# Destination one-hots kept in DRAM by two passes and loaded by two later ones, in a four-layer graph network

## The chip, the cores and the metric

The kernel runs on one core of a Trainium2 chip. The metric is the device time of one execution in microseconds. Engines: PE (TensorE, matmuls, with its weight loads shown apart as PEld), DVE (VectorE), ACT (ScalarE), POOL (GpSimd), SP (SyncE, which issues the DMAs).

## What is computed

The input is a graph of 12,500 nodes and 200,000 edges (`src`, `dst`, a type and a weight per edge) and a 64-wide feature `x` per node. Four layers follow each other, each with a residual and a layer norm. Cut to what matters here:

```python
# layer 0: two hyperbolic hops over the edges (per-edge arithmetic, then a mean by src)
x = _layernorm(x + _L0_gnn_ref(x, relation_emb, edge_index, edge_type))
# layer 1: two rounds; messages are summed by src, from rows gathered by dst, then a GRU cell
agg = segment_sum(messages, row, N); x = gru_cell(agg, x, ...)
# layer 2: two SAGE convolutions, 16 wide inside; rows gathered by src, mean by dst
h   = relu(segment_sum(x[src], dst, N) * inv_deg @ W1_l + b1 + x @ W1_r)
out =      segment_sum(h[src], dst, N) * inv_deg @ W2_l + b2 + h @ W2_r
# layer 3: two SAGE convolutions, 64 to 128 to 64, the same gather and mean
```

So layers 1 to 3 are six sums over all edges: two that gather by dst and add by src (layer 1), four that gather by src and add by dst (layers 2 and 3).

## The kernel before, in words

The setup sorts the edges into a 49 x 49 grid. A cell (k, j) holds the edges whose summing node lies in group k and whose gathered node lies in group j (256 nodes to a group); each cell is one tile of at most 128 edges. There are 49 x 49 = 2401 tiles. For each tile two short vectors are kept: the gathered node's place as a row in DRAM (`d_rows`, `s_rows`) and the summing node's place as a column in SBUF (`slc` by src, `dlc` by dst, one column of 128 values per tile). Then come the two hops of layer 0 (L1332, `hyper_hop`), which also make one-hots: the first hop stores them in DRAM (L1366, L1451) and the second loads them (L1368, L1453).

The change lies in the six passes at the end (`sum_pass`, L1659), called at L1942 to L1947: passes 0 and 1 are layer 1, passes 2 and 3 layer 2, passes 4 and 5 layer 3. A pass walks the 2401 tiles in 172 steps of PG = 14 tiles (the last has 7). For each step `prepare` (L1669) does this:

- a DMA brings the rows of the 14 tiles, broadcast to all partitions (`row`, 448 KB, L1671);
- two DVE tensor_scalars compare them with the partition's number: `o`, the one-hots by gathered node, for each half of a group (L1676);
- one DVE tensor_tensor compares `iota_r` with the tiles' columns: `s`, the one-hots by summing node, [128, 256 nodes, 14 tiles] with the tile innermost (L1678).

PE uses them in two kinds of matmul. `gather` (L1682) multiplies `o` with the table of node values (kept in three bf16 parts, so 3 x 64 = 192 columns; in layer 2 3 x 16 = 48, or 49 with a count) into the PSUM tile `pg` (L1690), and ACT casts it to `gb` (L1696). `scatter` (L1699) multiplies a tile's `s` with its `gb` and adds into `ps`, one PSUM bank for each k (L1704). A gather block has 2 tiles with 192 columns and 7 tiles with 48 or 49; a scatter follows two blocks later, or one.

When the last tile of a k has been added, the node work of that k (a generator such as `gru_node`, L1769) goes into a queue, and `tick` (L1652) issues a piece of it every second time: DVE reduces `ps` (L1727), in layer 1 makes the second half of `u` (L1777), PE transposes (L1781), ACT copies and activates, and so on to the table of the next pass.

The order on PE, DVE, ACT and POOL is the order in which this Python code issues the instructions (`manual_schedule`, L1637). The order on SP, which issues all DMAs, is chosen by the framework's scheduler. `row`, `o` and `s` have two buffers each. The preparation of step i+1 is issued among the gathers of step i.

## Time and profile before

| | us |
|---|---|
| median of 3 runs (12247.88 to 12251.74) | 12251.63 |
| the profiled execution's own time | 12251.38 |
| its span in the trace | 12249.7 |
| layer 0 and setup, to the first gather of pass 0 | 7090.9 |
| passes 0 and 1 (layer 1) | 982 and 1131 |
| passes 2 and 3 (layer 2) | 610 and 697 |
| passes 4 and 5 (layer 3), to the end of the span | 926 and 813 |

The profile is one execution, taken by the hardware profiler. "Busy" is the time in which an engine works on at least one instruction. Consecutive instructions of DVE overlap a little in it, so an instruction's duration is somewhat longer than the time from its start to the start of the next. A wait is the idle time of an engine before an instruction, put down to the instruction that released it. The granted clock is the share of TensorE's full clock that the throttle allowed; over the whole execution it was 0.922. A name such as "o<-row,iota_p" says what an instruction writes and reads; L1676 is line 1676 of the kernel.

### The profile page before, as it was taken

Reading aid. Unit: us, or ns where it says so; the run is one execution under the profiler, and the core shown is the slowest. Engines: PE = TensorE matmul, PEld = TensorE weight load, DVE = VectorE, ACT = ScalarE, POOL = GpSimd, SP = SyncE. Lnnn points to the kernel's source line nnn. Section 1 sums busy time; section 2 is a strip of 40 time slices with the busy share of each in tenths; the row PEclk is TensorE's granted clock in tenths of the full one; section 3 lists DMA queues with packets and bytes.
Section 4 is the critical chain, followed back from the end, with each engine's and each line's share of the span. In section 5 each row is a group of like instructions: output and inputs, shape, how many; then the busy total and the mean of one; then the engine's idle time right before and its main releaser. Section 6 shows DMA issues by size and latency. Waiting matters only on the chain.

```text
span 12249.7 us, 360176 instructions
## 1 busy us (share of the span) xinstructions
PE 10426.3 (85%) x147935; PEld 9021.3 (74%) x147935; DVE 9997.8 (82%) x22903; ACT 8238.9 (67%) x22338; POOL 1120.3 (9%) x2806
## 2 busy tenths in 40 slices
PE   6865888888888489999999689999997777999999
PEld 5754666666666377777777479988887777899999
DVE  7877999999999687787777676666669999766788
ACT  4544777777777488888888656667773222566777
POOL 0002222222222011111111000000000000000000
PEclk8777999999999799999999899999997766899999
DMA  1127777777677555555555422222223333222232
GB/s 30 11 27 232 262 263 262 265 262 265 262 264 263 132 213 212 211 210 213 211 212 212 135 78 83 81 76 70 72 70 123 136 116 115 95 88 87 96 105 97
DMA packets 681163, 1903.34 MB, mean 155 GB/s; under 512 B 324353, under 2 KB 327016, under 8 KB 591687
## 3 DMA queue, kind: packets, MB, share of 16 engines
q1 hardware_dynamic: 679494, 1880.19, 44.8%
q8 instruction: 1158, 18.97, 0.6%
q14 instruction: 511, 4.18, 0.1%
HBM read 1294.39 MB, written 585.58 MB: 153 GB/s over the span
## 4 chain that ended last, share of the span: by engine, by line
PE 43%; DVE 38%; ACT 11%; issue 6%; DMA 2%; SPq 0%; ACTq 0%; DVEq 0%; POOL 0%
PE ps L1704 13%; PE pg L1690 12%; DVE q L1407 5%; PE pm L1429 4%; DVE hd L1410 3%; DVE s L1678 3%; DVE o L1676 3%; ACT RS L1424 2%; PE ph L1376 2%; DVE z L1182 2%; ACT L1182 2%; PE po L963 2%; ACT mx L1437 2%; DVE oh L1449 2%; PE ps L1461 2%
## 5 line engine op out<-in xcount | busy, mean ns | idle before, releaser
L1696 ACT CAST gb<-pg 128x384 bf16<-128x384 f32 (+2 forms) x5490 | 2550.4, 474 | 1567.4 <-PE pg L1690 1555.3
L1704 PE MATMUL ps<-gb,s 128*128 128x192 bf16 (+2 forms) x28812 | 3070.3, 240 | 207.7 <-ACT gb L1696 196.3
L1690 PE MATMUL pg<-xs,o 128*128 128x192 bf16 (+2 forms) x28812 | 2849.5, 232 | 156.7 <-DMA row<-d_rows 125.7
L1704 PEld LDWEIGHTS <-s 128*128 128x128 bf16 x28812 | 2529.4, 146 | 277.0 <-issue 246.0
L1690 PEld LDWEIGHTS <-o 128*128 128x128 bf16 x28812 | 2070.8, 102 | 177.8 <-issue 129.9
L1676 DVE TENSOR_SCALAR o<-row,iota_p 128x1792 bf16<-128x1792 f16 x2064 | 1369.2, 681 | 653.4 <-PE pg L1690 643.3
L1376 PEld LDWEIGHTS <-o 128*128 128x128 bf16 x28812 | 1093.4, 100 | 1069.3 <-issue 476.6
L1376 PE MATMUL ph<-hx,o 128*128 128x69 bf16 x28812 | 1166.4, 199 | 685.1 <-DVE o L1363 314.1
L1678 DVE TENSOR_TENSOR s<-iota_r,dlc 128x3584 bf16<-128x3584 f16 x688 | 1391.5, 2023 | 184.1 <-PE ps L1704 183.3
L1437 ACT ACTIVATE mx<-pm 128x448 bf16<-128x448 bf16 x2058 | 1117.7, 544 | 579.3 <-PE pm L1440 574.8
L1424 ACT ACTIVATE HS<-HS,wh 128x64 f32<-128x64 f32 x4802 | 1225.9, 358 | 1.0 <-DVE wh L1182 1.0
L1424 ACT ACTIVATE RS<-RS,wtr 128x64 f32<-128x64 f32 x4802 | 1217.7, 341 | 0.0
L1382 PEld LDWEIGHTS <-o 128*128 128x128 bf16 x28812 | 1082.5, 100 | 115.2 <-issue 60.2
L1382 PE MATMUL pt<-tabx,o 128*128 128x67 bf16 x28812 | 1107.2, 198 | 2.1 <-issue 2.1
L1461 PE MATMUL ps<-mx,oh 128*128 128x196 bf16 (+1 forms) x9604 | 968.1, 254 | 0.0
L1678 DVE TENSOR_TENSOR s<-iota_r,slc 128x3584 bf16<-128x3584 f16 x344 | 696.1, 2024 | 245.6 <-PE ps L1704 243.6
L1461 PEld LDWEIGHTS <-oh 128*128 128x128 bf16 x9604 | 849.1, 134 | 46.1 <-issue 28.8
L1410 DVE TENSOR_REDUCE hd<-q 128x7 f32<-128x448 f32 x1372 | 823.1, 613 | 0.0
L1429 PE MATMUL pm<-HS,ident 128*128 128x448 f32 x1372 | 685.8, 581 | 93.7 <-ACT mx L1437 93.3
L1440 PE MATMUL pm<-mx,nident 128*128 128x448 bf16 x1372 | 498.7, 363 | 249.0 <-ACT mx L1437 249.0
L1429 PE MATMUL pm<-T,ident 128*128 128x448 f32 x1372 | 628.8, 539 | 0.0
L1429 PE MATMUL pm<-RS,ident 128*128 128x448 f32 x1372 | 627.4, 538 | 0.6 <-ACT RS L1424 0.6
(377 smaller groups left out, 15335.7 us busy)
## 6 DMA issues: line engine op xcount, KB each, us to landing
by_node<-o SPq DMA_DIRECT2D x343, 1120.0 KB
o<-by_node SPq DMA_DIRECT2D x343, 1120.0 KB
row<-s_rows SPq DMA_DIRECT2D x684, 448.0 KB
row<-hop_rows SPq DMA_DIRECT2D x343, 672.0 KB
by_edge<-oh SPq DMA_DIRECT2D x343, 448.0 KB
oh<-by_edge SPq DMA_DIRECT2D x343, 448.0 KB
row<-d_rows SPq DMA_DIRECT2D x342, 448.0 KB
heads<-hx SPq DMA_DIRECT2D x14, 724.5 KB
```

What stands on the lines that cost most here:

```text
L1376: pe.matmul(ph[:, t, :], o[:, 2 * q, t, :], head[k][:, q, i * RW : (i + 1) * RW], start=q + i == 0, stop=q + i == 3)
L1382: pe.matmul(pt[:, t, :], o[:, 2 * q + 1, t, :], tabx[:, 2 * (g * HG + t) + q, i * TW : (i + 1) * TW], start=q + i == 0, stop=q + i == 3)
L1410: vec.tensor_reduce(o, q[:, i], AX.X, OP.add)
L1424: act.mul(x[:, t, :], x[:, t, :], coef[k][2 * rels][:, g * HG + t : g * HG + t + 1])
L1429: pe.matmul(pm[n], ident, x, start=i == 0, stop=i == 2, skip_group_check=True)
L1437: act.activation(mx[n][:, :, i * D : (i + 1) * D], x, AF.Relu)
L1461: pe.matmul(ps[k][:, q, :], oh[n][:, q * P : (q + 1) * P, t], mx[n][:, t, :], start=g + t + q == 0, stop=g * HG + t == HT - 1, skip_group_ ...
L1676: ts(o[:, q, :n, :], row[:, :n, :], iota_p[:, q : q + 1], None, OP.is_equal)
L1678: tt(s[:, :, :n], iota_r[:, :, :n], cols_flat[:, t0 : t0 + n].unsqueeze(1).to_broadcast([P, GN, n]), OP.is_equal)
L1690: pe.matmul(pg[:, t, :], o[:, q, jo, :], xs[:, 2 * j + q, 0:wx], start=q == 0, stop=q == 1)
L1696: act.copy(gb[:, : len(js), :], pg[:, : len(js), :])
L1704: pe.matmul(ps[k][:, h, :], s[:, h * P : (h + 1) * P, jo], gb[:, t, :], start=j + h == 0, stop=j == NG - 1, skip_group_check=True)
```

## The change

In passes 0 and 1 a second generator, `keep_one_hots`, runs beside the gathers, one piece per tile. For each k it makes one-hots by destination for the tiles of column k of the later passes' grid that lie in the first seven of their step of 14; pass 0 makes every second one of them and pass 1 the others. Each is one DVE tensor_scalar of 128 x 256 (nodes innermost) with a column of `dlc` as the scalar. Up to four of them are stored by one DMA into `kept`, a DRAM tensor of 172 steps x 128 x 7 x 256.

In passes 2 and 3 (`load=True`) the first seven tiles of each step come from `kept` by one DMA of 448 KB, and only the other seven are made by the tensor_tensor. Passes 4 and 5 make all of them, as before.

In every pass `s` is now laid out in two blocks of seven tiles: a made block is [256 nodes, 7 tiles] with the tile innermost, a loaded block [7 tiles, 256 nodes] with the node innermost. `iota_r` has 7 instead of 14 columns per node, and the tensor_tensor that makes two blocks is one instruction with four dimensions.

```diff
-    iota_r = keep.tile([P, GN, PG], F16, name="iota_r")
+    iota_r = keep.tile([P, GN, HG], F16, name="iota_r")
...
+    iota_n = keep.tile([P, GN], F16, name="iota_n")
+    kept = dram.tile([-(-NG * NG // PG), P, HG, GN], BF16, name="kept")
...
-            s = wp.tile([P, GN, PG], BF16, name="s")
-            ready.append((o, s))
+            s = wp.tile([P, 2, GN * HG], BF16, name="s")
+            by_tile = s[:, 0, :].rearrange("p (t n) -> p t n", n=GN)
+            by_node = s.rearrange("p b (n t) -> p b n t", t=HG)
+            def edges_of(t, h):
+                hs = slice(h * P, (h + 1) * P)
+                return by_tile[:, t, hs] if load and t < HG else by_node[:, t // HG, hs, t % HG]
+            ready.append((o, edges_of))
+            if load:
+                m = min(n, HG)
+                nc.sync.dma_start(out=by_tile[:, :m, :], in_=kept[t0 // PG, :, :m, :])
             for q in range(2):
                 ts(o[:, q, :n, :], row[:, :n, :], iota_p[:, q : q + 1], None, OP.is_equal)
                 yield
-            tt(s[:, :, :n], iota_r[:, :, :n], cols_flat[:, t0 : t0 + n].unsqueeze(1).to_broadcast([P, GN, n]),
-               OP.is_equal)
+            b0, b1 = (1 if load else 0), n // HG
+            if b1 > b0:
+                c = cols_flat[:, t0 + b0 * HG : t0 + b1 * HG].rearrange("p (b t) -> p b t", t=HG)
+                tt(by_node[:, b0:b1], iota_r.unsqueeze(1).to_broadcast([P, b1 - b0, GN, HG]),
+                   c.unsqueeze(2).to_broadcast([P, b1 - b0, GN, HG]), OP.is_equal)
             yield
+
+        def keep_one_hots(k):
+            odd = k % PG >= HG
+            js = range(odd, NG, 2)[keep_half::2]
+            cols = wp.tile([P, NG], F32, name="cols")
+            copy(cols, dlc[:, :, k])
+            yield
+            for i in range(0, len(js), 4):
+                jj = js[i : i + 4]
+                d = wp.tile([P, 4, GN], BF16, name="d")
+                for t, j in enumerate(jj):
+                    ts(d[:, t, :], iota_n, cols[:, j : j + 1], None, OP.is_equal)
+                    yield
+                at = [(j * NG + k) // PG for j in jj]
+                nc.sync.dma_start(out=kept[at[0] : at[-1] + 1 : PG, :, k % HG, :].rearrange("s p n -> p s n"),
+                                  in_=d[:, : len(jj), :])
...
+                if keep_half is not None and j == 0:
+                    side.append(keep_one_hots(k))
+                while side and next(side[0], side) is side:
+                    side.pop(0)
...
-                    pe.matmul(ps[k][:, h, :], s[:, h * P : (h + 1) * P, jo], gb[:, t, :],
+                    pe.matmul(ps[k][:, h, :], s(jo, h), gb[:, t, :],
...
-    sum_pass(0, tabs[0], d_rows, slc, D, gru_node(0))
-    sum_pass(1, tabs[1], d_rows, slc, D, gru_node(1))
-    sum_pass(2, tabs[0], s_rows, dlc, 16, first_mean, extra=1)
-    sum_pass(3, tabs[1], s_rows, dlc, 16, second_mean)
+    sum_pass(0, tabs[0], d_rows, slc, D, gru_node(0), keep_half=0)
+    sum_pass(1, tabs[1], d_rows, slc, D, gru_node(1), keep_half=1)
+    sum_pass(2, tabs[0], s_rows, dlc, 16, first_mean, extra=1, load=True)
+    sum_pass(3, tabs[1], s_rows, dlc, 16, second_mean, load=True)
```

## The prediction

> **What bounds it now.** I read the page for the costliest groups, cut the six summing passes apart by counting the gather's weight loads (4802 to a pass), and took the windows view over these stretches, passes 0 to 5 in order. Columns: microseconds, busy time of PE, weight loads, VectorE (DVE), ScalarE (ACT), GpSimd; granted clock, DMA share, GB/s.

> ```profile
> core 0: us, PE busy (x) PEld busy (x) DVE busy (x) ACT busy (x) POOL busy (x), PEclk, DMA share, GB/s
> 7090.90:8073.00 982.10, 963.83 (x10755) 921.47 (x10756) 668.29 (x945) 634.60 (x1536) 0.00 (x0) 1.00 0.24 82
> 8073.00:9204.00 1131.00, 1021.60 (x11059) 965.49 (x11058) 731.51 (x1468) 816.35 (x1822) 0.00 (x0) 0.99 0.21 71
> 9204.00:9814.00 610.00, 482.88 (x9647) 468.13 (x9644) 587.23 (x943) 171.25 (x463) 0.00 (x0) 0.77 0.39 131
> 9814.00:10511.00 697.00, 547.68 (x9900) 527.60 (x9898) 635.60 (x1048) 204.16 (x581) 0.00 (x0) 0.66 0.34 115
> 10511.00:11437.00 926.00, 904.30 (x10190) 869.39 (x10190) 635.81 (x773) 624.28 (x1498) 0.00 (x0) 1.00 0.26 87
> 11437.00:12249.70 812.70, 798.87 (x9617) 795.04 (x9614) 681.80 (x1010) 587.30 (x1305) 0.00 (x0) 1.00 0.31 101
> ```

> Passes 0, 1, 4, 5 are held by PE (98, 90, 98, 98% busy; DVE 65 to 84%). Passes 2 and 3, where a matmul moves only 48 or 49 columns, are held by DVE (96 and 91%); PE is at 79% there. So DVE time taken from passes 2 and 3 counts nearly in full, and DVE time put into passes 0 and 1 costs only where PE waits for DVE. The waits view of pass 0 shows how much room DVE has there (total us, times, longest):

> ```profile
> DVE o L1676 <- PE pg L1690: 186.2, 123, 2.1
> DVE s L1678 <- PE ps L1704: 114.5, 147, 1.5
> ```

> 301 us in 172 steps, 1.75 us a step.

> **Part 1: the one-hot `s`.** The page's group for s, and the same operation in the first hop with rows of 7 (source view: ns min/median/max):

> ```profile
> L1678 DVE TENSOR_TENSOR s<-iota_r,dlc 128x3584 bf16<-128x3584 f16 x688 | 1391.5, 2023 | 184.1 <-PE ps L1704 183.3
> ```
> ```profile
> L1449 DVE TENSOR_TENSOR oh<-iota_r,slc x343: 1154/1218/1239, 1108.1 to 4104.9; 128x1792 bf16<-128x1792 f16 x172
> ```

> Rows of 14 cost 2023 ns for 3584 elements, rows of 7 cost 1218 for 1792, the same types and broadcasts. So a block of seven costs more than half. The changed program has 684 full-width s (two blocks) in passes 0, 1, 4, 5, 342 half-width ones in passes 2 and 3 and none in their last step. In passes 2 and 3: 342 x (2.023 - 1.218) = **276 us less DVE**. A two-block s: twice 1.218 less one start of an instruction. The smallest DVE rows (128x2) take about 0.15, so 2.29, **0.26 more than now**; bounds 0 and 0.41 (2 x 1.218). 171 a pass: 45 us of DVE in each of passes 0, 1, 4, 5.

> [...]

> **Part 2: the kept one-hots, made.** 1204 tensor_scalars 128x256 with a column as scalar, 602 a pass, 12 or 13 for each k, and 98 copies of 49 columns. The same operation in two widths:

> ```profile
> L1364 DVE TENSOR_SCALAR o<-row,iota_p 128x1792 bf16<-128x1792 f16 x343 | 233.8, 682 | 0.0
> ...
> L1365 DVE TENSOR_SCALAR o<-row,iota_f 128x896 bf16<-128x896 f16 x343 | 154.2, 450 | 0.0
> ```

> (682 - 450)/896 = 0.259 ns an element; at 256 wide 450 - 640 x 0.259 = 284 ns, and queued instructions start 0.085 before the last has ended (below: 0.69 long, 0.60 to the next start): **0.20 each**, bounds 0.07 (start-to-start of 128x2 rows) and 0.28. The copy: 0.1. With s that is 120 + 5 + 45 = 170 us of DVE a pass, 1.0 a step. On average it fits into 1.75. It does not come on average: all 13 stand in the first 14 of a k's 49 tiles, beside the first pieces of the last k's node work. The timeline there, pass 0:

> ```profile
> 7192.25 0.69 DVE L1676 TENSOR_SCALAR o<-row,iota_p 128x1792 bf16<-128x1792 f16 x1
> 7192.85 0.55 DVE L1727 TENSOR_REDUCE u<-ps 128x128 f32<-128x384 f32 x1
> ...
> 7194.12 2.02 DVE L1678 TENSOR_TENSOR s<-iota_r,slc 128x3584 bf16<-128x3584 f16 x1
> ...
> 7196.06 0.28 DVE L1777 TENSOR_TENSOR u<-X 128x128 f32<-128x128 f32 x1
> ...
> 7196.40 0.33 PE L1781 MATMUL n<-ident,u 128*128 128x128 f32 x1 [0.67 <-DVE u L1777]
> ```

> PE itself stands still for u, which DVE reaches behind s. In pass 0 PE's transpose starts 0.05 us after u's end in every second k and 0.25 in the others: there is no slack. In the changed order, every second k has the copy and 12 one-hots between 7191.22 (c, L1809) and u, with DVE waits of 0.46 in that stretch: 0.1 + 12 x 0.2 + 0.26 - 0.46 = 2.3 us later. The others have 11, with about 0.8 of waits and 0.25 of slack: 0.1 + 2.2 + 0.26 - 1.05 = 1.5. 49 x 1.9 = **+92 us in pass 0**. In pass 1, 24 k have slack 0 and more waits ahead of u (about 1.8), 25 have slack 1.45: 0.9 and 0.5 each, 34 us; PE also waits 96 us for ACT's casts there, which hides some: **+25**. Bounds for both passes 20 (the waits swallow all) and 200 (0.28 each, nothing hidden).

> Where u is late, what is queued behind it on PE is the whole stream of gathers and scatters; on ACT it is the casts gb behind the copies of the node.

> **The stores.** 322 DMAs, up to four tiles (256 KB in 512-byte pieces). The buffer d has two copies, so the first one-hot of the third group waits for the first group's store. No such store is in this trace. A row load of 448 KB takes 3.2 us from its issue to its last packet (median in pass 0, from the trace's packets), and 512-byte packets took 27 ns, 0.9 us for 512 on 16 engines, so 2.6 to 4 us against about 2.1 to 3.7 of DVE work between: 0 to 1 us a k, **+10**, bounds 0 and 90. On SP the stores are queued among the row loads; the changed order keeps two or three row loads ahead of them, so rows still come a step early.

> **Part 3: the loads in passes 2 and 3.** 344 loads of 448 KB. Their DMA time, 1.2 us of all engines each (the hop's one-hot loads of that size), beside a row's 1.35: 2.55 us a step of 3.55 or 4.05. A load may start when the scatter of two steps before has ended and must land before the next scatter on that buffer: two steps are at least the landing + a scatter block, a gather block, a scatter block (about 2.0). At 3.3 that is 2.65 us a step; DVE then needs 2.6 (pass 2) and 2.9 (pass 3). The loops are about equally long, so not all 276 come back.

> PE gets a little from it. Weight loads in pass 2, fourteen of each:

> ```profile
> 9502.15 0.51 PEld L1690 LDWEIGHTS <-o 128*128 128x128 bf16 x14
> 9502.58 0.93 PEld L1704 LDWEIGHTS <-s 128*128 128x128 bf16 x14
> ```

> o is read contiguously, s with a step of 14 elements. The loaded half becomes contiguous: up to 0.42 a step on PE, 72 us a pass (bounds 0 and that). With the other passes' 192 columns (0.33 us for four matmuls of either kind) no weight load shows.

> [...]

> Pass 2: DVE 587 - 138 = 449, PE 483 - 67 = 416, landing 172 x 2.65 = 456. Three loops this close do not overlap fully; I take 88% for DVE: 510, **-100**. Pass 3: 636 - 138 = 498, at 87%: 572; its node chains through ACT stay, so 582, **-115**. Bounds for both: -276, and +10 (landing 5.5).

> Passes 4, 5: DVE +45 each; waits of 285 us in pass 4 take it, but 25 k there already hold PE up at their transposes (23 us): 25 x 0.26 = 7, and 5 for pass 5, whose DVE goes to 89%. **+12**, bounds 0 and 40.

> **Sum** against the profiled execution, 12251.4 (span 12249.7; median of the runs 12251.6): -215 + 92 + 25 + 10 + 12 = -76, **12175**.

> **Rivals.**
> *The load takes the place of the one-hot (slower).* In the second hop the one-hot loads, behind 1120 KB loads in the same queue, ended 4.9 us after their issue. If the row load in the queue ahead does the same here, a step is (4.9 + 2.1)/2 = 3.5 and at 5.5 it is 3.8, what it is now on average (1307/344). The gain is 0 to 110, the 139 stay: 12280 to 12390, say **12320**. It decides from a landing of about 4.9 on. Against it: no row load in pass 2 took that long (90% under 3.65).
> *The waits swallow the one-hots.* 301 us of waits in pass 0 and 307 in pass 1 are more than 170: cost 20, **12070**. Against it: no slack at u.
> *DVE stalls on the stores*, at 4 us and one-hots of 0.28: 220 in passes 0 and 1, **12265**.
> That the change does not do what it says is ruled out by the order: the instructions are there.

> **Chances.** Forecast 0.47 (12110 to 12225), load 0.24, swallowed 0.14, stores 0.15. Range 12060 to 12330. About 0.2% (25 us) is what a measurement tells from no change. Faster: forecast 0.45, swallowed 0.14, a little of the others, 0.63. Same: mostly the stores, 0.15. Slower: 0.22.

> **What would show it.** s at 1.2 us in passes 2, 3 and 2.3 elsewhere; the small one-hots at 0.28 long; the wait of PE's transposes for u in pass 0 up from 0.9 to about 2 us a k; pass 2 near 510, pass 3 near 582, passes 0 and 1 near 1080 and 1160. Wrong if scatters in passes 2, 3 wait for the load of s, or if PE in pass 0 waits no more than now.

## The result and the profile after

The changed kernel takes 12520.03 us in the median of 4 runs (12513.23 to 12529.17), the kernel before beside it 12250.88 (12247.88 to 12251.74): 1.022 times as long, 95% interval 1.0208 to 1.0232. The forecast was 12175. The span of the profiled run is 12523.2 us, 273.5 longer than before. The windows view of the changed kernel, cut at the same places (columns: us, busy time of PE, weight loads, DVE, ACT, GpSimd; granted clock, DMA share, GB/s):

```profile
7091.40:8284.70 1193.30, 1033.57 (x10755) 978.59 (x10756) 840.74 (x1610) 640.27 (x1536) 0.00 (x0) 0.94 0.33 101
8284.70:9521.30 1236.60, 1064.26 (x11059) 998.39 (x11058) 899.28 (x2105) 819.74 (x1822) 0.00 (x0) 0.96 0.31 96
9521.30:10125.40 604.10, 432.76 (x9649) 412.82 (x9648) 458.10 (x943) 174.73 (x463) 0.00 (x0) 0.64 0.80 263
10125.40:10766.70 641.30, 487.31 (x9899) 460.69 (x9896) 506.90 (x1047) 202.29 (x581) 0.00 (x0) 0.63 0.75 247
10766.70:11701.60 934.90, 905.21 (x10193) 869.93 (x10189) 677.98 (x772) 623.76 (x1498) 0.00 (x0) 1.00 0.26 86
11701.60:12523.20 821.60, 799.10 (x9620) 795.06 (x9617) 720.37 (x1010) 586.88 (x1305) 0.00 (x0) 1.00 0.31 100
```

| pass | before | forecast | after | after less before |
|---|---|---|---|---|
| 0 | 982 | about 1080 | 1193 | +211 |
| 1 | 1131 | about 1160 | 1237 | +106 |
| 2 | 610 | 510 | 604 | -6 |
| 3 | 697 | 582 | 641 | -56 |
| 4, 5 | 926, 803 | +12 | 935, 810 | +16 |

(The last pass ends with the last scatter here; the window above runs to the end of the span.) Read the busy columns against the time. In passes 2 and 3 VectorE has lost nearly what was forecast, 129 us in each (587 to 458 and 636 to 507; forecast 138), and the time has not followed: neither it nor TensorE (PE) is busy for more than four fifths of the stretch now, and the DMA share has gone from 0.39 to 0.80. In passes 0 and 1 TensorE's own busy time is up by 70 and 43 us, though it executes the same matmuls, and its clock is down from 1.00 and 0.99 to 0.94 and 0.96. The prices of the single instructions came out as forecast (groups of the changed kernel, shapes apart: busy us, mean ns, idle before):

```profile
L1695 DVE TENSOR_TENSOR s<-iota_r,dlc 128x3584 bf16<-128x3584 f16 x342 | 783.6, 2291 | 130.2 <-PE ps L1743 124.2
...
L1695 DVE TENSOR_TENSOR s<-iota_r,dlc 128x1792 bf16<-128x1792 f16 x344 | 419.7, 1220 | 62.5 <-PE ps L1743 62.2
...
L1710 DVE TENSOR_SCALAR d<-iota_n,cols 128x256 bf16<-128x256 f16 x1204 | 285.7, 281 | 71.9 <-DMA kept<-d 68.2
```

2.29, 1.22 and 0.28 us were forecast as 2.29, 1.218 and 0.284. So it is the waits that went wrong. Pass 0 of the changed kernel (total us, times, longest):

```profile
PE n L1823 <- DVE u L1819: 150.7, 48, 5.2
...
DVE s L1695 <- PE ps L1743: 115.4, 114, 2.6
...
DVE d L1710 <- DMA kept<-d: 46.5, 62, 2.5
```

In the kernel before, TensorE waited a ninth of that for u in pass 0:

```profile
PE n L1781 <- DVE u L1777: 16.1, 24, 0.7
```

And pass 2 of the changed kernel:

```profile
PE ps L1743 <- DMA s<-kept: 124.9, 99, 3.3
DVE o L1690 <- DMA row<-s_rows: 108.8, 85, 3.5
```

Both engines wait for transfers there. Before, no s was loaded, and the waits for row came to 0.2 us in passes 2 to 5 together. The timeline of pass 2 shows one turn of it (start, duration; the bracket is the idle time before and who ended it):

```profile
9699.59 0.32 SPq L1688 DMA_DIRECT2D s<-kept  x1
9699.67 0.68 DVE L1690 TENSOR_SCALAR o<-row,iota_p 128x1792 bf16<-128x1792 f16 x1
...
9700.38 0.32 SPq L1675 DMA_DIRECT2D row<-s_rows  x1
...
9703.03 0.91 PE L1743 MATMUL ps<-gb,s 128*128 128x49 bf16 x14
...
9703.97 0.32 SPq L1688 DMA_DIRECT2D s<-kept  x1
...
9705.63 0.77 PE L1743 MATMUL ps<-gb,s 128*128 128x49 bf16 x14 [1.11 <-DMA s<-kept]
...
9706.82 1.28 DVE L1690 TENSOR_SCALAR o<-row,iota_p 128x1792 bf16<-128x1792 f16 x2 [1.07 <-DMA row<-s_rows]
```

The row load leaves at 9700.38, 0.03 us after the o that frees its buffer has ended (9699.67 + 0.68); it has landed at 9706.72 and the o that needs it starts at 9706.82. The load of s that leaves at 9699.59 lands at 9705.58, and the scatter starts at 9705.63. Of the 16 parts of that load, 15 had landed by 9703.05 (by the trace's semaphore updates): the last part alone cost 2.5 us.

Landing times, from issue to the last of the 16 parts, median and the 10 and 90% points, worked out from those updates:

| | row, pass 2 | s, pass 2 | row, pass 3 | s, pass 3 |
|---|---|---|---|---|
| before | 3.55 (3.33 to 4.19) | none | 3.53 | none |
| after | 5.09 (4.42 to 6.23) | 4.50 (3.81 to 5.61) | 4.65 | 4.16 |

Before, a row had been there 1.9 us when its o started (median of pass 2). After, in 67% of pass 2's steps the o starts within 0.15 us of the landing.

The scatter at 9705.63 starts 0.05 us behind the sixteenth part and 2.6 behind the fifteenth: in this turn it began only when the last part had landed.

### The profile page after: what moved, and what is told of

Its sections match the earlier page's. It is cut to its first block, busy times and chain, and to the rows that moved or that the text cites. A ratio compares the mean times of both kernels' runs of the same rounds, so it can differ in the third digit from the quotient of the medians.

```text
span 12523.2 us, 363233 instructions
## 1 busy us (share of the span) xinstructions
PE 10435.4 (83%) x147935; PEld 8993.4 (72%) x147935; DVE 10156.3 (81%) x24203; ACT 8249.6 (66%) x22338; POOL 1107.2 (9%) x2807
## 4 chain that ended last, share of the span: by engine, by line
PE 36%; DVE 34%; ACT 10%; DMA 9%; issue 4%; SPq 0%; DVEq 0%; ACTq 0%; POOL 0%
PE ps L1743 11%; PE pg L1725 10%; DVE q L1407 5%; PE pm L1429 4%; DMA row<-s_rows 4%; DVE hd L1410 3%; DVE s L1695 3%; DMA kept<-d 2%; ACT RS L1424 2%; PE ph L1376 2%; DVE z L1182 2%; ACT L1182 2%; ACT mx L1437 2%; DVE oh L1449 2%; DMA s<-kept 2%
## 5 line engine op out<-in xcount | busy, mean ns | idle before, releaser
L1743 PE MATMUL ps<-gb,s 128*128 128x192 bf16 (+2 forms) x28812 | 2985.4, 239 | 320.6 <-DMA s<-kept 169.6
L1725 PE MATMUL pg<-xs,o 128*128 128x192 bf16 (+2 forms) x28812 | 2918.1, 236 | 139.6 <-DMA row<-d_rows 125.9
L1743 PEld LDWEIGHTS <-s 128*128 128x128 bf16 x28812 | 2369.6, 133 | 416.9 <-DMA s<-kept 209.9
L1725 PEld LDWEIGHTS <-o 128*128 128x128 bf16 x28812 | 2127.7, 104 | 156.9 <-issue 129.6
L1690 DVE TENSOR_SCALAR o<-row,iota_p 128x1792 bf16<-128x1792 f16 x2064 | 1369.1, 680 | 746.9 <-PE pg L1725 565.7
L1376 PEld LDWEIGHTS <-o 128*128 128x128 bf16 x28812 | 1094.2, 100 | 1066.6 <-issue 476.8
L1695 DVE TENSOR_TENSOR s<-iota_r,dlc 128x1792 bf16<-128x1792 f16 (+1 forms) x686 | 1203.2, 1754 | 192.7 <-PE ps L1743 186.4
L1382 PEld LDWEIGHTS <-o 128*128 128x128 bf16 x28812 | 1082.0, 100 | 114.8 <-issue 59.9
L1695 DVE TENSOR_TENSOR s<-iota_r,slc 128x3584 bf16<-128x3584 f16 x344 | 785.6, 2284 | 230.0 <-PE ps L1743 229.6
```

What stands on the lines that cost most here:

```text
L1376: pe.matmul(ph[:, t, :], o[:, 2 * q, t, :], head[k][:, q, i * RW : (i + 1) * RW], start=q + i == 0, stop=q + i == 3)
L1382: pe.matmul(pt[:, t, :], o[:, 2 * q + 1, t, :], tabx[:, 2 * (g * HG + t) + q, i * TW : (i + 1) * TW], start=q + i == 0, stop=q + i == 3)
L1690: ts(o[:, q, :n, :], row[:, :n, :], iota_p[:, q : q + 1], None, OP.is_equal)
L1695: tt(by_node[:, b0:b1], iota_r.unsqueeze(1).to_broadcast([P, b1 - b0, GN, HG]), c.unsqueeze(2).to_broadcast([P, b1 - b0, GN, HG]), OP.is_e ...
L1725: pe.matmul(pg[:, t, :], o[:, q, jo, :], xs[:, 2 * j + q, 0:wx], start=q == 0, stop=q == 1)
L1743: pe.matmul(ps[k][:, h, :], s(jo, h), gb[:, t, :], start=j + h == 0, stop=j == NG - 1, skip_group_check=True)
```

## The theories

*The first theory*, formed on these views: in passes 0 and 1 the kept one-hots stand ahead of u, and TensorE stands still for it; its clock drops from standing. In passes 2 and 3 the two transfers of a step share the DMA engines and land late, and two loops set the step: two steps are a landing of row and the two o's after it, and two steps are a landing of s and two scatters. *The rivals*: the layout in rows of seven; the stores, by the waits for d or by their traffic; SP's order (a load or store stands behind another that waits); the DMA engines simply being full.

All kernels below are edits of the changed kernel, and their passes are cut in the same way. But for the last two, each time is that of one execution. Where two of them have the same code in a pass, it takes the same time within 6 us in passes 0 and 1, within 4 in passes 4 and 5, and from 590 to 604 us in pass 2; differences under that are not read.

## The experiments

**The layout alone.** Nothing is kept or loaded:

```diff
-    sum_pass(0, tabs[0], d_rows, slc, D, gru_node(0), keep_half=0)
+    sum_pass(0, tabs[0], d_rows, slc, D, gru_node(0))
 ...
-    sum_pass(3, tabs[1], s_rows, dlc, 16, second_mean, load=True)
+    sum_pass(3, tabs[1], s_rows, dlc, 16, second_mean)
```

> The one-hots s in blocks of seven in all six passes, nothing kept and nothing loaded: the layout alone. The first theory (most of the loss of passes 0 and 1 is VectorE work put ahead of u, and passes 2 and 3 lose their gain to late transfers) expects the layout to cost only its 0.26 us an s: where VectorE holds the step, passes 2 and 3, 171 x 0.26 = 45 each (655 and 740 us), where TensorE waits for u, 49 x 0.26 = 13 in pass 0 (995) and less in pass 1 (1137), 9 and 7 in passes 4 and 5 as the changed kernel shows them; in all about 12370. The rival that the layout itself is what costs in passes 0 and 1 (its reads by TensorE, or s behind which u stands) expects pass 0 at 1090 or more and pass 1 at 1180 or more.

Measured 12366.89 (12252.87 before beside it). Windows of passes 0 to 3:

```profile
7088.80:8084.30 995.50, 964.62 (x10755) 920.73 (x10756) 713.27 (x945) 635.16 (x1536) 0.00 (x0) 1.00 0.24 81
8084.30:9223.30 1139.00, 1022.56 (x11060) 965.22 (x11058) 776.16 (x1468) 817.51 (x1822) 0.00 (x0) 0.99 0.21 70
9223.30:9875.50 652.20, 474.54 (x9648) 449.13 (x9647) 632.68 (x944) 171.44 (x463) 0.00 (x0) 0.68 0.37 123
9875.50:10610.30 734.80, 529.93 (x9898) 503.80 (x9896) 679.75 (x1047) 202.15 (x581) 0.00 (x0) 0.61 0.33 109
```

995, 1139, 652, 735, and 933 and 812: every pass about as the 0.26 us an s says (171 x 0.26 = 45 where VectorE holds the step, measured 42 and 38). Rows of seven cost 13 and 8 us in passes 0 and 1; they are not where 211 and 106 went. From 652 and 735 the loads bring 48 and 94 us.

**Made and stored, not loaded.** `load=True` is taken out of passes 2 and 3 alone.

> As the changed kernel, but passes 2 and 3 make all of s and load nothing; the one-hots are still made and stored in passes 0 and 1. Both theories expect passes 0 and 1 at 1193 and 1237 us, as in the changed kernel (if not, the loads reach back into them). In passes 2 and 3 the first theory expects what the layout alone gives, 655 and 740, granted clock near 0.75 and 0.65, row transfers landing in 3.2 us again and no wait of VectorE for row; then the loads brought 50 and 100 us, and the rest of the 276 went into waits for row and s. The rival that the row transfers are late for another reason than the loads expects waits for row here too.

Measured 12672.5: 1199 and 1242 us in passes 0 and 1, 652 and 735 in 2 and 3, row landing in 3.55 us again (median) and no waits for row. The lateness of row comes with the loads of s, and the loads cost passes 0 and 1 nothing. So a row with a load of s in flight beside it lands later, after 5.09 us and not 3.55; what the two share that does it is not shown, nor what a load of s would take alone.

**Made, not stored.** The same, without the two lines that issue the store; the one-hots in d go nowhere.

> As the one before (nothing loaded), and without the stores: the kept one-hots are made into d and go nowhere, so the 322 transfers and the waits of d for them are gone, and VectorE's work is the same. The first theory (the work ahead of u) expects pass 0 at 1145 to 1180 and pass 1 at 1215 to 1230: less than the changed kernel by no more than the waits of d, 46 and 22 us. The rival that the stores hold VectorE (they are 14 and 11 per cent of the chain of waits in passes 0 and 1) expects pass 0 near 1060 and pass 1 near 1130.

Measured 12489.92: 1083 and 1176 us. Both theories miss: the stores cost 115 us in pass 0 and 66 in pass 1, far more than the waits of d. Windows of pass 0 with and without the stores, the kernel with them first:

```profile
7089.90:8288.50 1198.60, 1039.23 (x10756) 984.08 (x10757) 840.84 (x1610) 641.65 (x1536) 0.00 (x0) 0.93 0.33 101
```
```profile
7090.20:8173.70 1083.50, 968.93 (x10756) 920.82 (x10757) 835.16 (x1610) 634.08 (x1536) 0.00 (x0) 1.00 0.22 74
```

and TensorE's wait for u, in the same order:

```profile
PE n L1823 <- DVE u L1819: 150.5, 48, 5.3
```
```profile
PE n L1819 <- DVE u L1815: 106.3, 48, 2.9
```

These account for 114 of the 115 us: the wait for u is up by 44 us (the waits of d, 46, handed on), and TensorE's busy time by 70, with the clock at 0.93 where it was 1.00. Without stores the one-hots' own work costs 88 us over the layout's 995, nearly all of it the wait for u (22.5 to 106.3).

What the 70 us are, the timeline of the kernel with the stores shows:

```profile
7318.52 0.33 PE L1823 MATMUL n<-ident,u 128*128 128x128 f32 x1 [3.41 <-DVE u L1819]
...
7319.02 0.49 PE L1743 MATMUL ps<-gb,s 128*128 128x192 bf16 x4
...
7337.42 0.49 PE L1725 MATMUL pg<-xs,o 128*128 128x192 bf16 x4
7340.26 0.33 PE L1823 MATMUL n<-ident,u 128*128 128x128 f32 x1 [2.35 <-DVE u L1819]
...
7340.80 0.85 PE L1743 MATMUL ps<-gb,s 128*128 128x192 bf16 x4
...
7343.36 0.85 PE L1743 MATMUL ps<-gb,s 128*128 128x192 bf16 x4
...
7344.39 0.49 PE L1743 MATMUL ps<-gb,s 128*128 128x192 bf16 x4
```

After the stand of 2.35 us four matmuls take 0.85 us, not 0.49, for 3.4 us; after the longer stand of 3.41 us, one k earlier, they take 0.49. The granted clock in the records falls from 1.0 to 0.5 at 7340.70 and is back at 7344.11. All such changes lie on a grid of 3413.3 ns (fitted to the 320 of this kernel's six passes, none off by over 0.6 ns). I took each window of that grid in pass 0 and worked out, from the starts and ends of the matmuls in the trace (the ends are modelled), which share of it TensorE stood still. In the kernel with the stores: of 20 windows at full clock that were idle for 0.30 to 0.55 of their length none was followed by one at half, of 4 between 0.55 and 0.60 two, of 34 over 0.60 all. Without the stores no window was idle for over 0.55, and the clock did not fall once. The stand of 2.35 us lies in one window and leaves it idle for 0.69; the one of 3.41 us is cut by a border and leaves two windows idle for 0.50 each. Eight stands of 3.41 to 3.44 us in this pass lie like that (no window idle for over 0.57) and were not followed by a fall. So a stand that is a little longer can cost once more, in a step: that is why the stores cost more than their waits.

**One-hots twice, no stores.** The kernel without stores, with each kept one-hot made two times:

```diff
-                    ts(d[:, t, :], iota_n, cols[:, j : j + 1], None, OP.is_equal)
+                    for _ in range(2):
+                        ts(d[:, t, :], iota_n, cols[:, j : j + 1], None, OP.is_equal)
```

> Nothing stored and nothing loaded; each kept one-hot is made twice, in the changed kernel's place, so that u comes later by VectorE's work alone. Without the doubling pass 0 takes 1083 us, TensorE waits 106 us for u (1.5 and 2.9 us in turn), is busy 969 us and its clock is 1.00. The doubling puts some 9 to 11 more one-hots of 0.2 us ahead of u: 2 us a k, 100 us. The theory that TensorE's clock drops after a stand of more than about 3 us (with the stores: 48 stands of 2.1 to 5.3 us, 36 of them with a stretch at half the clock behind them, TensorE busy 70 us more) expects a clock of 0.95 or less, TensorE busy 1020 or more and pass 0 at 1240 to 1290. The rival (the stores' traffic slows TensorE) expects the clock at 1.00, TensorE busy 969 and pass 0 at 1180 to 1200.

Measured 13055.37; pass 0:

```profile
7092.50:8468.30 1375.80, 1082.17 (x10755) 1022.64 (x10756) 1011.58 (x2226) 644.22 (x1536) 0.00 (x0) 0.86 0.18 59
```

The clock falls to 0.86 and the busy time rises by 113 us with a DMA share of 0.18: no store is needed for it. The wait for u, 283 us, is more than I had put (stands of 6.8 us in every second k, of 5.1 in the others), so 1376 and not 1240 to 1290. Against the kernel without the doubling VectorE is busy 176 us more, the wait for u is 177 longer and TensorE's busy time 113: the last two are 290 of the 292 us. The mechanism is shown; a border at 3 us is not (2.35 us above was followed by half the clock, eight stands of 3.41 to 3.44 us were not), and the size was not foreseen: an added one-hot came through to TensorE with all of its 0.29 us, not with 0.2.

**Stores from another queue.** `nc.sync.dma_start` of the store becomes `nc.gpsimd.dma_start`, nothing loaded.

> Nothing loaded; the one-hots made at the start of each k and stored as in the changed kernel, but the stores issued from GpSimd's queue. On SP a store stands behind a row load that waits for VectorE (SP's queue waits 462 us for o in pass 0), and the store then ends up to 4.4 us after its issue could have come. The theory that the place in SP's order makes the stores cost 116 us in pass 0 and 66 in pass 1 expects no waits of d, the wait for u at 106 us, the clock at 1.00, pass 0 at 1083 to 1105 and pass 1 at 1176 to 1195. The rival (the transfer itself is too long, or its traffic slows TensorE) expects pass 0 at 1150 or more, pass 1 at 1215 or more and a clock under 0.97.

Measured 12734.56: 1236 and 1268 us, worse. Pass 0:

```profile
7088.50:8324.40 1235.90, 1058.11 (x10755) 1001.37 (x10756) 840.66 (x1610) 641.84 (x1536) 128.17 (x175) 0.91 0.30 98
```

The stores land 2.8 us after their issue from there (2.36 from SP), and d waits 73 us, not 46. Since they also land later, this run alone does not rule SP's order out. The trace of the kernel with the stores does: there each store of pass 0 leaves SP within 0.28 us of the end of its last one-hot, 0.03 in the median (0.29 from GpSimd). SP's order holds no store up.

**Stores in twos, from four buffers.** The same space for d, but a buffer comes round after six one-hots and not after four:

```diff
-            for i in range(0, len(js), 4):
-                jj = js[i : i + 4]
-                d = wp.tile([P, 4, GN], BF16, name="d")
+            for i in range(0, len(js), 2):
+                jj = js[i : i + 2]
+                d = wp.tile([P, 2, GN], BF16, name="d", bufs=4)
```

> Nothing loaded; the one-hots at the start of each k as in the changed kernel, and stored from SP, but in groups of two from four buffers and not of four from two, in the same space: a buffer comes round after six more one-hots and not after four. The theory (VectorE's waits for the stores, 46 us in pass 0, lengthen TensorE's stands for u from at most 2.9 us to 5.3, and a 3.41 us window of TensorE that stands idle for more than about 0.57 of it is followed by one at half the clock) expects no waits of d, u waiting 106 to 120 us, a clock of 0.98 to 1.00, pass 0 at 1083 to 1105 us and pass 1 at 1176 to 1195. The rival (the stores' own traffic or their number on SP costs the 116 and 66 us) expects pass 0 at 1150 or more and pass 1 at 1215 or more.

Measured 12541.75: 1118 and 1189 us. The waits of d are 10 us in pass 0, the wait for u 113, the clock 0.97. That is between the two ranges in pass 0, 80 of the stores' 115 us gone; in pass 1 it is within the theory's range. The remaining 35 us are the 28 by which TensorE's busy time is still above that without stores (12 windows idle for over 0.6 of it are left) and 7 of wait for u; what makes some stands up to 3.6 us long, where none was over 2.9 without stores, is not settled.

**The one-hots behind u.** They begin at tile 14 of a k, one for each second tile; the work and the stores are the same:

```diff
-                if keep_half is not None and j == 0:
+                if keep_half is not None and j == 14:
                     side.append(keep_one_hots(k))
-                while side and next(side[0], side) is side:
+                while side and j % 2 == 0 and next(side[0], side) is side:
```

> The changed kernel, with the kept one-hots of a k begun at its tile 14 and not at tile 0, one for each second tile, so that they come behind u, with the same stores and the same work for VectorE. The first theory expects the transposes of pass 0 to wait for u about as before (20 to 40 us in the pass), pass 0 at 990 to 1020 and pass 1 at 1140 to 1165, and the granted clock of both back at 0.99 or 1.00; the whole 12170 to 12250. The rival that VectorE's 170 us a pass cost wherever they stand (or that the stores do) expects pass 0 at 1140 or more and pass 1 at 1200 or more. Passes 2 to 5 stay as in the changed kernel: 604, 641, 935, 810.

Measured 12209.91, with 12252.87 before beside it:

```profile
7088.40:8083.90 995.50, 964.65 (x10756) 920.84 (x10757) 838.08 (x1610) 635.19 (x1536) 0.00 (x0) 1.00 0.39 122
8083.90:9224.00 1140.10, 1024.04 (x11059) 966.79 (x11058) 891.84 (x2105) 817.67 (x1822) 0.00 (x0) 0.99 0.34 105
9224.00:9814.00 590.00, 418.60 (x9648) 398.18 (x9646) 458.43 (x943) 174.32 (x463) 0.00 (x0) 0.70 0.82 269
```

The wait for u in pass 0 is what it is with the layout alone:

```profile
PE n L1823 <- DVE u L1819: 22.5, 24, 0.9
```

Passes 0 and 1 take what the layout alone takes, 995 and 1140, with 1204 one-hots and 322 stores more: VectorE's 125 us in pass 0 and all of the stores' traffic are free behind u. Where and how densely the same work stands decides 294 us in these two passes (the whole went from 12520 to 12210). The edit moves the one-hots and also spreads them, one for each second tile; no run separates the two.

**Loads from another queue**, the one-hots spread: `nc.gpsimd.dma_start` for the load of s.

> The kernel with the one-hots spread, and with the loads of passes 2 and 3 issued from GpSimd's queue and no longer from SP's between the row loads. In the spread kernel a row load leaves SP within 0.05 us of the end of the o that frees its buffer and a load of s right behind the scatter that frees its buffer, so the first theory (the two transfers of a step share the DMA engines and land late, 4.4 to 5.1 us in the median and the last of the 16 parts later still, against 3.55 for a row alone) expects nothing from the queue: passes 2 and 3 at 580 to 600 and 630 to 650 us. The rival (one queue in order: row is late because it stands behind the load of s) expects row landing in 3.6 us again, pass 2 at 540 or less and pass 3 at 600 or less. Passes 0, 1, 4, 5 as in the spread kernel: 995, 1140, 935, 810.

Measured 12291.45: 649 and 663 us in passes 2 and 3. Both miss, the rival in its direction too. The waits for row fall to 12 us, but row lands in 4.9 us still; the loads of s land in 5.0 (4.4 from SP), their first part 3.7 after the issue and not 2.9, and the scatters wait 177 us for them. By the waits the loop of s takes the place of the loop of row: (5.0 + 2.0)/2 = 3.5 us a step, of the 3.8 that pass 2 takes. The other 0.3 are not explained.

**The second block loaded**, the one-hots spread. `by_tile` is `s[:, 1, :]`, VectorE makes block 0, and the parity of the kept tiles is turned round.

> The kernel with the one-hots spread, with the second block of seven of each step kept and loaded and not the first, so that a load of s has about half a step more before its scatter. The first theory (loops of one landing and two steps) expects the wait of the scatter for the load to go (122 us in pass 2 of the spread kernel) and the loop over row to stay, two steps less 1.3 us for a landing of 5 us, 3.15 to 3.3 us a step: pass 2 at 545 to 575, pass 3 at 600 to 630. The rival (the DMA engines are full at 80 per cent and 270 GB/s) expects 590 and 639, the waits moved to row. Passes 0, 1, 4, 5 at 995, 1140, 935, 810.

Measured 12291.79: 613 and 695 us. The scatter's wait for the load is gone (122 to 9 us), as the theory has it, and the time is up, which neither said: row still lands in 5.0 us, and now o, and what VectorE does behind it, holds TensorE (65 us for o) and ScalarE (227 us for H, a tensor of the node work, 139 in the spread kernel). That this is why the time is up is read from the waits, not tested.

**Three buffers for row**, the one-hots spread. To make room, the one-hots are also stored one by one, from three small buffers, and gb has three buffers and not four; the line for row:

```diff
-            row = wp.tile([P, PG, P], F16, name="row")
+            row = wp.tile([P, PG, P], F16, name="row", bufs=3)
```

> The kernel with the one-hots spread, with three buffers for row and not two (room made by storing the one-hots one by one from three small buffers, and by three buffers for gb and not four). In the spread kernel a row load leaves at the end of the o that frees its buffer, lands 5.0 us later in pass 2, and in 71 per cent of the steps the o that needs it starts 0.1 us after that: two steps are 0.03 + 5.0 + 0.1 + 1.35 for the o's = 6.5 of the measured 6.8 us. The theory that this loop sets passes 2 and 3 expects the waits for row to go with the third buffer, and the loop of s next, (4.4 + 2.0) / 2 = 3.2 us a step: pass 2 at 545 to 575 us, pass 3 at 595 to 630. The rival (the DMA engines are full: 82 per cent, 269 GB/s) expects the landing to grow as loads start earlier, and 585 to 595 and 635 to 645. Passes 0 and 1 stay at 995 and 1140 if 1204 small stores cost no more than 322 large ones.

Measured 12195.85: 554 and 616 us, both within the theory's ranges, though the row loads land no sooner (5.1 us). Pass 2:

```profile
9269.90:9823.80 553.90, 403.90 (x9649) 384.66 (x9648) 460.11 (x943) 177.98 (x463) 0.00 (x0) 0.75 0.84 286
```

The waits for row are gone, and the next loop shows (waits of pass 2):

```profile
PE ps L1743 <- DMA s<-kept: 127.2, 118, 3.5
DVE s L1695 <- PE ps L1743: 75.0, 109, 2.4
```

(4.1 + 2.0)/2 = 3.05 us a step for that loop; the pass takes 3.2. Full DMA engines are ruled out as the bound at 590: the share is 0.84 at 554. The single small stores do cost: 1035 us in pass 0, with 158 us of waits of d.

**Both**, three buffers for row (with the small stores and the three gb) and the second block loaded.

> As the kernel with three buffers for row, and with the second block of seven loaded and not the first, which took the scatter's waits for the load from 122 us to 9 and left row as the last. The theory of the two loops expects neither to bind: VectorE's 458 us at 90 per cent or the 484 us of DMA work at 95 per cent set pass 2, 500 to 530 us, and pass 3 is 575 to 615. The rival (full DMA engines) expects 560 or more and 620 or more, with a DMA share of 0.85 or less and landings of 5.5 us or more.

Measured 12170.25: 582 and 573 us. Pass 3 comes out just under the theory's range of 575 to 615, pass 2 far over its 500 to 530: row still ends waits there (101 us; landing 5.2), and H holds ScalarE (169). Here the rival's 560 or more holds in pass 2, at a share of 0.81. What sets pass 2 in this form is open.

**Rows of 14 again where nothing is loaded**, the one-hots spread, with the small stores and the three gb, and two buffers for row.

> The kernel with the one-hots spread, with s in rows of 14 again in the four passes that load nothing, as in the kernel before; rows of 7 in passes 2 and 3 alone. The layout alone cost 13, 8, 7 and 9 us in passes 0, 1, 4 and 5, so the theory expects 982, 1131, 926 and 803 there and passes 2 and 3 as they were, 590 and 639: 12165 to 12180 in all. The rival that reading iota_r with a step (rows of 7 out of 14) slows the half-width s of passes 2 and 3 expects it above 1.23 us and passes 2 and 3 longer by 171 times the difference.

Measured 12212.71: 1007, 1132, 602, 641, 928, 803. Three of the four passes that load nothing are as before the change; the half-width s takes 1.221 us with an `iota_r` of 14 columns too; pass 0 has 25 us over 982, where the single stores make d wait 173 us.

**Together.** The one-hots spread, stored in twos from three buffers, rows of 14 in passes 0, 1, 4, 5, three buffers for row, and single buffers for node work to make room; with the first and with the second block loaded.

> What the runs so far say to mend, together: the one-hots spread over tiles 14 to 42 of a k, stored in twos from three buffers; s in rows of 14 again in passes 0, 1, 4 and 5; three buffers for row in passes 2 and 3; the room for it from single buffers for u, fa, fb, fc, rz, c, q and n_q of the node work. If the parts add up: 982, 1131, 554, 616, 926 and 803 us, 12100 to 12140 in all, 0.988 to 0.991 of the kernel before. The rival (the parts hinder each other: node work on single buffers, stores among the rows) expects over 12160.

> As the run before it, with the second block of seven kept and loaded. Pass 2 was 582 and pass 3 573 us so, against 554 and 616: 12085 to 12125 in all, some 15 us under the other, if the parts add up; over 12160 if they hinder each other.

Measured 12119.12 (0.9896 of before, interval 0.988 to 0.9913) and 12107.26 (0.9881, 0.9865 to 0.9897): the parts add up, and which block is loaded can't be told apart by these intervals. Windows of the second of them, passes 0 to 3:

```profile
7090.60:8073.20 982.60, 964.01 (x10755) 921.62 (x10756) 795.80 (x1603) 635.53 (x1536) 0.00 (x0) 1.00 0.40 123
8073.20:9204.20 1131.00, 1021.46 (x11060) 965.43 (x11059) 848.10 (x2105) 817.38 (x1822) 0.00 (x0) 0.99 0.34 105
9204.20:9796.10 591.90, 418.85 (x9649) 391.45 (x9648) 457.15 (x944) 175.16 (x463) 0.00 (x0) 0.75 0.81 267
9796.10:10377.00 580.90, 460.09 (x9895) 437.50 (x9894) 503.11 (x1048) 203.84 (x581) 0.00 (x0) 0.70 0.82 273
```

Passes 0 and 1 are as if nothing were made or stored. Both take about 1% less time than the kernel before, and 3% less than the changed one. Of the forecast 215 us in passes 2 and 3, this one brings 610 + 697 - 592 - 581 = 134. That a load of half the bytes would land sooner was not tried.

## Why the forecast was wrong

The sum was -76 and came out at +272, 348 us more. Two steps failed: the term for the stores, by 171 us, and the step time with the loads, by 153. The forecast's own sign of being wrong is in the profile: the scatters of passes 2 and 3 wait for the load of s (125 us in pass 2). TensorE's wait for u in pass 0 grew as it said, but to 3.1 us a k and not to about 2.

- **Part 1, s.** Right: 2.29 and 1.22 us. Rows of seven do cost more per element than rows of 14 (1220 ns for 1792 is 0.68 each, 2023 for 3584 is 0.56), as the hop's row had it. The cost in the passes that load nothing, 13, 8, 9 and 7 us, is what 0.26 an s gives.
- **Part 2, the kept one-hots.** "49 x 1.9 = +92 us in pass 0", with +25 in pass 1: measured without stores 101 and 45 (with the layout's 13 and 8). The right mechanism, 29 us too little, most of it in pass 1.
- **Part 2, the stores.** "+10, bounds 0 and 90": measured 181 (115 and 66). This step failed. Its waits were within its bound (46 and 22 us of d), and I let them end there. They are ahead of u like the one-hots, so they lengthen the same stands, and the stands turned long enough for the clock to fall (1.00 to 0.93): 70 us of slower matmuls in pass 0 that stood in no term. I had read the clock in the windows, 1.00 in pass 0 and 0.66 to 0.77 where TensorE stands often, and not asked what the longer stands would do to it.
- **Part 3, the loads.** "At 3.3 that is 2.65 us a step": the landing is 4.5 us for s, and 3.55 becomes 5.09 for row. This step failed, in size and in one loop left out. I took the landing of a row alone, and that only to its last packet (to the sixteenth part it was 3.55), for the landing of two transfers in flight together, and worked out the loop of s only. Row's own loop, two steps = 0.03 + 5.09 + 0.10 + 1.35, is 3.3 a step and was the last in two thirds of them; its cover, 1.9 us before the change, was not put against a later landing. Instead of -215, -62. That row's loop held the step is shown by the third buffer (590 to 554 us); with s also out of the way, what holds pass 2 at 582 and 592 us stays open.
- **The rival on the loads** had the right direction: 62 us came back, within its 0 to 110. That its 3.5 us a step for a landing of 4.9 is the measured 604/172 = 3.51 is partly luck: s landed after 4.5 us, which by its sum is 3.3, row's loop is not in it, and the order in the queue, its reason, is not what makes the loads late (from another queue s landed in 5.0 us, and row still in 4.9). What spoke against it, that no row took so long, was read from a trace in which row was alone, and to the last packet; to the sixteenth part nine of the 171 took over 4.9 us there too.
- **The rival on the stores**, 220 us in passes 0 and 1, fell short (317 there, 181 of it from the stores), and by another way: it counted waits of VectorE, and the larger part, 118 of the 181 us as slower matmuls, is the clock.
- **PE's gain from whole weights** is there: scatters of 14 take 0.76 us from the loaded block and 0.91 from the made one, and TensorE is busy 42 us less in pass 2 than with the layout alone. It cannot show while transfers set the step.
- **Passes 4 and 5.** +12 forecast, +16 measured.
- **The rival that the waits swallow the one-hots** missed for this order (146 us without stores, not 20). But its numbers, 1.75 us of waits a step against 1.0 of new work, were sound: in the spread kernel passes 0 and 1 pay for the layout alone. Only the place and the spacing were wrong.

## What to carry to other kernels

Work for an engine with slack costs by its place (here the same work took 294 us less in passes 0 and 1 behind u and spread out): look for what the bound engine waits for on it, and put new work behind that and spread out, not ahead of it in one piece. A transfer that was added lengthened those that were there (row from 3.55 to 5.09 us in pass 2): work out each loop of a buffer (landing plus use, over the number of buffers), the old ones too, with a landing for the transfers together. Where the bound engine is TensorE, price a stand twice, once for itself and once for the clock after it (44 and 70 us here, for the stores in pass 0).
